# Two graph layers on one core: the second adjacency's exchange moved into the last slots of h1's tile, and the start-up order around it

## The chip, the cores and the metric

The kernel runs on one core of one Trainium2 chip. The metric is device time in microseconds for one execution over the whole batch of 32 graphs; lower is better. The core's engines appear as PE (matrix multiply), PEld (its weight load), DVE (vector), ACT (scalar, activation), POOL (GpSimd) and SP (which here only issues DMAs). Each engine works through its own list of instructions in the order in which the program wrote them; semaphores hold an instruction back until what it needs is there.

## What is computed

For each of 32 graphs with 512 nodes and 512 features, in float32:

```python
h = max(layernorm(x), 0)
agg = (adj @ h) / max(adj.sum(-1), 1e-6)
x = x + relu(concat([h, agg]) @ W.T)            # layer 0
h1 = max(layernorm(x), 0)
q, k = split(h1 @ Wqk); v = h1 @ Wv
w = rowsum(q * (adj @ (k * mask))) * mask / sqrt(512)
x = x + softmax(w over the nodes) * v            # layer 1
```

## The kernel before

Every 512 x 512 product is made with seven products of 256 x 256 quarters instead of eight (Strassen's scheme in Winograd's form). A function `product` emits them in the order M1, M2, M6, M5, M7, M3, M4. One such M with one pair of operands is a **block** of eight matmuls on PE. Each operand is a tile of seven slots: four quarters, and three sums which DVE makes in place with four additions (`left_sums`, `right_sums`; sum 0 fills slot 4, sum 1 slot 6, sum 2 slot 5, sum 3 rewrites a quarter). M1 and M2 need quarters alone; M6 is the first that needs a sum (slot 5).

The stages of a graph b are:

- **y_b** (`layer0_y`): h times the second half of W; seven blocks, result Y.
- **o_b** (`layer0_out`): h times the first half of W, plus adj times Y; each M has two blocks (first h with a streamed weight tile `w1`, then aT with Y), 14 blocks in all.
- **u_b** (`layer1_u`): adj times the masked h1; seven blocks, result U.
- **tv** (`layer1_tv`): h1 times the joined weights of layer 1.

An operand that has to be turned is normalized or scaled on ACT, written to DRAM by row chunks (four DMAs), read back by an **exchange** (four DMAs for each half: `sh..`, `sa..` tiles from the `s` buffers, of which there are two) and then turned on DVE (`turn`). For adj the turned tile is `aT`, for h `hT`, for h1 `h1T`. The tile `aT` is one buffer, shared by all graphs: the first half of its turn (quarters 0 and 1) can be written once M1 and M2 of the stage before have read them, the second half after M4.

The order is written out by hand. `run(phase, n, plan)` emits one block, then the functions that the plan holds under this step's number, then goes on with the product's own code. So a copy or an addition that belongs to an M is emitted after the plan of the step in which its block was emitted. For example, in u the copy of M5's bank (`m5`) is emitted after the plan of step 3 and before M7; in o, with two blocks an M, the copy of M7's bank comes after the plan of step 9. PE accumulates M7 and M4 into the bank `pp`, and M5 and M3 into `pq`: M4 waits for the copy of M7's bank, and M3 for that of M5's.

Four short buffers (`block`, tag `tmp`) hold `m5` and other scratch. In y_1 they also hold the four normalized chunks of graph 0's h1 (`write` in `start`), in the order chunk 0, chunk 1, m5, chunk 2, chunk 3.

The diff touches the start-up: graph 0's stages, written out in `start`, and the first turn of the loop that follows (i = 1: the stage o_1). The pieces to know are:

- `late`, the start's scratch in the buffer of h1T (7 x 7 x 128 per partition): early operands of the weight product, the mask, an identity.
- `fb`, graph 1's adjacency (`FrontA(1)`): loaded and scaled in o_0, chunks written at steps 9 to 12, exchange and first turn in u_0, second turn at step 0 of o_1.
- `f`, graph 0's h1 (`FrontH1(0)`): exchange in y_1, turned and summed in u_0.
- `fd`, graph 2's x (`FrontH(2)`): loaded at step 13 of o_0 into the two `n` half tiles that `fb` leaves, statistics at step 0 of u_0, then `shift` (DVE, makes the bias of the normalization) and `write` (ACT normalizes, SP issues the DMA).
- `fa` in the loop, graph 2's adjacency (`FrontA(2)`): `load`, `sum` (ACT, row sums), `degrees` (DVE), `write`.
- `weights`: additions of 128 x 1792 on the joined weights of layer 1, needed by the stage tv.
- SP issues nearly all DMAs, in the order of emission.

Of the kernel before, what the change touches and what calls it, by code (L numbers as in the profile page):

```python
# [11 lines left out]
F32 = mybir.dt.float32  # L12
# [4 lines left out]
P = 128  # L17
# [5 lines left out]
def kernel(  # L23
# [13 lines left out]
    C = N // P  # L37
# [7 lines left out]
    big = ctx.enter_context(tc.tile_pool(name="big", bufs=1))  # L45
# [43 lines left out]
    def right_sums(s, on=None):  # L89
        return [  # L90
            lambda: sub(s(4), s(1), s(0), on), lambda: sub(s(6), s(3), s(1), on),
            lambda: sub(s(5), s(3), s(4), on), lambda: sub(s(1), s(2), s(5), on),
        ]

    def of(t):
        return lambda i: t[:, i]
# [68 lines left out]
    def run(phase, n, plan):  # L165

        for i in range(n):
            if phase is not None:
                next(phase)
            for f in plan.get(i, []):  # L170
                f()
        if phase is not None:
            assert next(phase, "end") == "end"
# [32 lines left out]
    def exchange(src, name, t=None, queues=one_queue):  # L206


        if t is None:
            t = big.tile([P, 8, P], F32, tag="s", bufs=2, name=name)  # L210
        for q in range(Q):
            queues[q % 2].dma_start(
                out=t[q * R:(q + 1) * R, :, :], in_=src[:, :, ts(q, P)].rearrange("k r j -> r k j")
            )
        return t
# [5 lines left out]
    X, AT_, DEG, W, Y, H1M, H1T, U, TV, HT = ({} for _ in range(10))  # L221
# [44 lines left out]
    def halves(d):  # L266

        return d.rearrange("(h c) (q r) j -> h (c q) r j", h=2, q=Q)

    class Turned:  # L270
# [10 lines left out]
        def turn(self, h, dst):  # L281
            o = dst[:, 2 * h:2 * h + 2, :, :].rearrange("p a b (k r) -> p k (a b) r", r=R)
            nc.vector.transpose(o, self.s.pop(h).rearrange("p k (c r) -> p k c r", r=R))
# [73 lines left out]
    class FrontH1:  # L357
# [30 lines left out]
            right_sums(of(H1M[self.b]))[i]()  # L388

        def turn(self, h):  # L390
            if h == 0:
                H1T[self.b] = big.tile([P, 7, 7, P], F32, tag="h1T", bufs=1, name=f"h1T_{self.b}")
            for a in range(2):
                self.to.turn_slot(h, a, H1T[self.b][:, 2 * h + a, 0:4, :].rearrange("p i f -> p (i f)"))
# [58 lines left out]
    def layer1_u(b):  # L453
        return product(f"u_{b}", [(AT_[b], right(H1M[b]))], *into(U[b]), seed=b + 1 == B)
# [316 lines left out]
    FH, FA, F1 = {}, {}, {}  # L771
# [5 lines left out]

    def start():

        late = big.tile([P, 7, 7, P], F32, tag="h1T", bufs=1, name="late").rearrange("p s i f -> p (s i f)")  # L780
        identity = held["identity"] = late[:, 5120:5248]
        make_identity(nc, identity)
        still = late[:, 5248:5248 + 512]
# [23 lines left out]
        fa = FA[0] = FrontA(0)  # L807
# [92 lines left out]
        p = Plan()  # L900
# [39 lines left out]
        weights = [right_sums(outer)[k] for k in range(4)] + [right_sums(inner)[k] for k in range(4)]  # L940
# [12 lines left out]
        fb = FA[1] = FrontA(1)  # L953
        p = Plan()
# [41 lines left out]
        p.at(11, fh.turn, 1)  # L996
        p.at(11, fh.sums, 0)
        p.at(11, fh.sums, 2)
        fd = FH[2] = FrontH(2)
        for h in range(2):  # L1000
            p.at(13, fd.load, h)
        f = F1[0] = FrontH1(0)
# [9 lines left out]
        p = Plan()  # L1012
# [23 lines left out]
        p = Plan()  # L1036
        for c in range(C):
            p.at(0, fd.stats, c)
        p.at(0, variance, fd.t)
        p.at(1, f.turn, 0)  # L1040
        p.at(1, fb.to.read, 0)
        p.at(1, f.turn, 1)
        p.at(1, fb.to.read, 1)
        p.at(1, load_x, 1)
        p.at(1, FA[0].factor)
        p.at(2, weights[6])
        r1 = right_sums(of(Y[1]))
        p.at(4, fb.turn, 0)
        p.at(4, r1[0])
        p.at(4, shift, fd.t)  # L1050
        p.at(4, r1[2])
        for c in range(C):
            p.at(5, fd.write, c)
        for k in range(4):
            p.at(5 + k // 2, f.sums, k)
        run(layer1_u(0), 7, p)
        return weights[7:], mv

# [4 lines left out]
    }  # L1063
    with tc.manual_schedule(engines=engines):
        weights, mvR = start()
        post = None
        for i in range(1, B):
            more, last = i + 1 < B, i + 1 == B
            f = F1[i] = FrontH1(i)
            p = Plan()  # L1070
# [12 lines left out]
                p.at(2 + 2 * (k // 2), right_y[k])  # L1083
            if i == 1:
                fa = FA[2] = FrontA(2)
                p.at(2, FH[2].to.read, 0)
                p.at(5, fa.load, 0)
                p.at(5, fa.load, 1)
                for h in range(2):
                    for c in range(2):  # L1090
                        p.at([9, 9, 10, 11][2 * h + c], fa.sum, 2 * h + c)
                        p.at(12 + h, fa.write, 2 * h + c)
                    p.at([10, 11][h], fa.degrees, h)
                for k, g in enumerate(weights):
                    p.at(6 + k, g)
                FH[3] = FrontH(3)
                p.at(13, FH[3].load, 0)
                p.at(13, FH[3].load, 1)
            f1 = F1[i - 1]
            if i > 1:  # L1100
                for k in range(4):
                    p.at(k // 2, f1.sums, k)
            if post is not None:
                for c in range(C):
                    p.at(2 + c, post.apply, c)
# [6 lines left out]
            if 1 < i and i + 2 < B:  # L1112
                fh = FH[i + 2]
                late = i == 2
# [12 lines left out]
            if 1 < i and i + 2 < B:  # L1127
                fa = FA[i + 2] = FrontA(i + 2)
# [8 lines left out]
            p = Plan()  # L1137
# [19 lines left out]
            if i == 1:  # L1157
                fa = FA[3] = FrontA(3)
# [32 lines left out]
            p = Plan()  # L1191
# [40 lines left out]
            if more:  # L1232
                p = Plan()
                fb = FA[i + 1]
# [24 lines left out]
        p = Plan()  # L1259
# [11 lines left out]
        p = Plan()  # L1271
# [39 lines left out]
```

## Time and profile before

| | |
|---|---|
| time, median of 3 runs | 2265.5 us (2265.22 to 2266.66) |
| time of the profiled execution | 2267.41 us |
| its span, first to last instruction | 2265.6 us |
| DVE busy | 1913.5 us (84%) |
| ACT busy | 1025.6 us (45%) |
| bytes moved by DMA | 463.69 MB, mean 205 GB/s |
| granted clock of PE | 1.000 over the span |

The span is that of the same execution as the 2267.41 us; 1.8 us lie around it. In a line of the timeline the columns are the start in us from the span's start, the duration in us, the engine (SPq is SP's queue of DMA issues), the source line, the operation, the output and the inputs by tile name, the number of merged instructions, and in brackets how long the engine had been idle just before and what ended it. In the view of waits the columns after the colon are total us, times, and longest us.

### The profile page before, as it was taken

What the parts mean: (1) busy time and instruction counts of PE and PEld (TensorE: products, weight loads), DVE (VectorE), ACT (ScalarE), POOL (GpSimd) and SP (SyncE); (2) the same over time, 40 slices, a digit from 0 to 9 for tenths busy, and PEclk for the clock granted to TensorE, in tenths of its full rate; (3) what the DMA queues carried; (4) which work ended last, traced back from release to release, by engine and by line L of the source; (5) the groups of instructions that cost most, each with busy time, mean ns of one, the idle gap of its engine ahead of it and who ended that gap; (6) DMA issues with size and microseconds to landing.
All of it is one profiled execution on the core that took longest, in us unless ns stands there. A gap on an engine that the chain in (4) does not pass through costs nothing.

```text
span 2265.6 us, 32862 instructions
## 1 busy us (share of the span) xinstructions
PE 2254.2 (99%) x10526; PEld 1981.4 (87%) x10526; DVE 1913.5 (84%) x3778; ACT 1025.6 (45%) x1895; POOL 176.7 (8%) x261
## 2 busy tenths in 40 slices
PE   9999999999999999999999999999999999999999
PEld 7888888888888888888888888888888888888888
DVE  7888888888888888888888888888888888888776
ACT  4364443445434554444454344543454443445323
POOL 0000000000010000000000000001000010000000
PEclk9999999999999999999999999999999999999999
DMA  9978777887878787778878788787778787787644
GB/s 205 252 220 240 210 210 194 204 233 205 210 199 200 214 224 204 203 196 208 229 205 210 193 203 223 218 210 198 193 213 228 203 210 193 206 231 207 155 122 107
DMA packets 409997, 463.69 MB, mean 205 GB/s; under 512 B 38208, under 2 KB 271680, under 8 KB 405600
## 3 DMA queue, kind: packets, MB, share of 16 engines
q1 hardware_dynamic: 396608, 426.46, 69.1%
q0 software_dynamic: 8928, 32.51, 8.6%
q10 hardware_dynamic: 4288, 2.62, 0.6%
q8 instruction: 83, 1.36, 0.3%
q14 instruction: 90, 0.74, 0.1%
HBM read 293.93 MB, written 167.51 MB: 204 GB/s over the span
## 4 chain that ended last, share of the span: by engine, by line
PE 95%; DMA 3%; DVE 1%; SPq 0%; ACT 0%; issue 0%; POOL 0%; DVEq 0%; ACTq 0%
PE ptv L470 28%; PE pp_o L103 19%; PE pp_u L103 9%; PE pq_o L103 9%; PE pp_y L103 9%; PE pq_u L103 5%; PE pr_o L103 5%; PE pq_y L103 5%; PE pr_u L103 2%; PE pr_y L103 2%; PE pw L521 1%; DMA w<-dw 0%; DMA mv<-in_L_gnn_Wqk_dram 0%; DMA mv<-in_L_gnn_W_dram 0%; DMA a<-in_adj_dram 0%; PE pp_v L103 0%
## 5 line engine op out<-in xcount | busy, mean ns | idle before, releaser
L470 PE MATMUL ptv<-mv,h1T 128*128 128x256 f32 x2940 | 639.4, 379 | 0.0
L470 PEld LDWEIGHTS ptv<-mv,h1T 128*128 128x128 f32 x2940 | 558.6, 190 | 75.9
L74 DVE TENSOR_TENSOR tv<-tv 128x256 f32<-128x256 f32 (+1 forms) x645 | 321.8, 511 | 13.2 <-ACT tv L80 1.5
L80 ACT ACTIVATE tv<-ptv 128x512 f32<-128x512 f32 (+1 forms) x360 | 185.0, 542 | 262.8 <-PE ptv L470 261.6
L103 PE MATMUL pp_u<-h1m,aT 128*128 128x256 f32 x1024 | 241.9, 379 | 0.0
L103 PE MATMUL pp_y<-wide 128*128 128x256 f32 x992 | 234.4, 379 | 0.7 <-ACT y L80 0.7
L103 PE MATMUL pp_o<-y,aT 128*128 128x256 f32 x992 | 234.3, 379 | 0.0
L103 PE MATMUL pp_o<-w,wide 128*128 128x256 f32 x960 | 226.8, 379 | 0.0
L103 PEld LDWEIGHTS pp_u<-h1m,aT 128*128 128x128 f32 x1024 | 194.5, 190 | 26.4
L103 PEld LDWEIGHTS pp_y<-wide 128*128 128x128 f32 x992 | 188.3, 190 | 26.6 <-ACT y L80 1.1
L103 PEld LDWEIGHTS pp_o<-y,aT 128*128 128x128 f32 x992 | 188.4, 190 | 25.6
L103 PEld LDWEIGHTS pp_o<-w,wide 128*128 128x128 f32 x960 | 182.4, 190 | 24.8
L80 ACT ACTIVATE o<-pp_o 128x512 f32<-128x512 f32 x96 | 57.2, 596 | 292.9 <-PE pp_o L103 287.7
L80 ACT ACTIVATE y<-pp_y 128x512 f32<-128x512 f32 x124 | 74.0, 597 | 234.0 <-PE pp_y L103 234.0
L74 DVE TENSOR_TENSOR tv<-ptv,tv 128x512 f32<-128x512 f32 x240 | 139.8, 614 | 43.1 <-PE ptv L470 39.4
L77 DVE TENSOR_TENSOR h1T<-h1T 128x512 f32<-128x512 f32 (+1 forms) x189 | 163.5, 878 | 1.3
L80 ACT ACTIVATE xu<-pp_u 128x512 f32<-128x512 f32 x127 | 75.8, 597 | 193.6 <-PE pp_u L103 193.6
L251 POOL TENSOR_TENSOR rstd<-rstd,mhalf 128x2 f32<-128x2 f32 (+1 forms) x97 | 80.0, 825 | 646.0 <-DVE rstd L250 635.6
L103 PE MATMUL pq_u<-h1m,aT 128*128 128x256 f32 x512 | 120.9, 379 | 0.0
L74 DVE TENSOR_TENSOR tv<-ptv,m_tv 128x512 f32<-128x512 f32 (+1 forms) x120 | 72.0, 622 | 57.0 <-PE ptv L470 56.6
L103 PE MATMUL pq_y<-wide 128*128 128x256 f32 x496 | 117.3, 379 | 0.0
L103 PE MATMUL pq_o<-y,aT 128*128 128x256 f32 x496 | 117.2, 379 | 0.0
(167 smaller groups left out, 3310.2 us busy)
## 6 DMA issues: line engine op xcount, KB each, us to landing
w<-dw SPq DMA_DIRECT2D x217, 256.0 KB, 4.3
a<-in_adj_dram SPq DMA_DIRECT2D x256, 128.0 KB, 3.0
dx<-xu SPq DMA_DIRECT2D x32, 1024.0 KB, 5.0
sh1T<-dh1T SPq DMA_DIRECT2D x256, 128.0 KB, 3.4
shT<-dhT SPq DMA_DIRECT2D x248, 128.0 KB, 5.8
daT<-a SPq DMA_DIRECT2D x124, 256.0 KB, 3.0
saT<-daT SPq DMA_DIRECT2D x248, 128.0 KB, 3.4
xu<-in_x_dram SPq DMA_DIRECT2D x124, 256.0 KB, 5.4
```

The costliest lines, as they stand in the source:

```text
L74: (on or nc.vector).tensor_tensor(o, a, b, op=ALU.add)
L77: (on or nc.vector).tensor_tensor(o, a, b, op=ALU.subtract)
L80: nc.scalar.activation(o, i, AF.Copy)
L103: nc.tensor.matmul(p[:, rc, :], lt[:, LEFT[k], dk, ts(rc, P)], right[:, dk, :], start=first and rc == 0 and dk == 0, stop=True, skip_group ...
L251: nc.gpsimd.tensor_tensor(rstd[:, a:b], rstd[:, a:b], mhalf[:, a:b], op=ALU.pow)
L470: nc.tensor.matmul(banks[n][:, :, ts(i, P)], left[:, LEFT[k], LEFT_IN[j], :], mvR[:, RIGHT[k], RIGHT[j], :, :], start=first and i == 0, st ...
L521: nc.tensor.matmul(banks[n][:, ts(i, P)], left[:, LEFT[k], LEFT_IN[j], :], mvR[:, RIGHT[k], RIGHT[j], which, :], start=first and i == 0, s ...
```

## The change

1. `late` becomes graph 0's h1T tile itself: it is made once, and h1's turn writes into it, without a new allocation.
2. The exchange of the second adj (`read_a`, 8 DMAs) moves from step 1 of u_0 to step 13 of o_0, ahead of `fd.load`, and lands in the last slots of that tile (its elements 3584 to 5631) instead of the `s` buffers.
3. h1's four sums, whose results go into these slots, move from u_0 (steps 5 and 6) to o_1 (steps 0 and 1), after the second turn of adj, which reads them free.
4. In u_0 the first turn of adj and `shift` go to step 2, ahead of the two turns of h1 (which go from step 1 to step 2); the four `fd.write` go from step 5 to step 3; `weights[6]` from step 2 to step 5.
5. In o_1 the read of graph 2's h goes from step 2 to 1, the first load of the third adj from step 5 to 3, its row sums from steps 9, 9, 10, 11 to 10, 10, 11, 11, and `degrees` from 10, 11 to 11, 12.

```diff
         def turn(self, h):
-            if h == 0:
+            if h == 0 and self.b > 0:
                 H1T[self.b] = big.tile([P, 7, 7, P], F32, tag="h1T", bufs=1, name=f"h1T_{self.b}")
...
-        late = big.tile([P, 7, 7, P], F32, tag="h1T", bufs=1, name="late").rearrange("p s i f -> p (s i f)")
+        H1T[0] = big.tile([P, 7, 7, P], F32, tag="h1T", bufs=1, name="late")
+        late = H1T[0].rearrange("p s i f -> p (s i f)")
...
+        def read_a(h):
+            room_a = late[:, 3584 + 1024 * h:3584 + 1024 * (h + 1)].rearrange("p (k f) -> p k f", f=P)
+            fb.to.s[h] = exchange(halves(fb.to.d)[h], f"saT_1_{h}", room_a)
+
+        for h in range(2):
+            p.at(13, read_a, h)
         fd = FH[2] = FrontH(2)
...
-        p.at(1, f.turn, 0)
-        p.at(1, fb.to.read, 0)
-        p.at(1, f.turn, 1)
-        p.at(1, fb.to.read, 1)
         p.at(1, load_x, 1)
         p.at(1, FA[0].factor)
-        p.at(2, weights[6])
         r1 = right_sums(of(Y[1]))
-        p.at(4, fb.turn, 0)
+        p.at(2, fb.turn, 0)
+        p.at(2, shift, fd.t)
+        for c in range(C):
+            p.at(3, fd.write, c)
+        p.at(2, f.turn, 0)
+        p.at(2, f.turn, 1)
         p.at(4, r1[0])
-        p.at(4, shift, fd.t)
         p.at(4, r1[2])
-        for c in range(C):
-            p.at(5, fd.write, c)
-        for k in range(4):
-            p.at(5 + k // 2, f.sums, k)
+        p.at(5, weights[6])
         run(layer1_u(0), 7, p)
...
-                p.at(2, FH[2].to.read, 0)
-                p.at(5, fa.load, 0)
+                p.at(1, FH[2].to.read, 0)
+                p.at(3, fa.load, 0)
                 p.at(5, fa.load, 1)
                 for h in range(2):
                     for c in range(2):
-                        p.at([9, 9, 10, 11][2 * h + c], fa.sum, 2 * h + c)
+                        p.at(10 + h, fa.sum, 2 * h + c)
                         p.at(12 + h, fa.write, 2 * h + c)
-                    p.at([10, 11][h], fa.degrees, h)
+                    p.at(11 + h, fa.degrees, h)
...
-            if i > 1:
-                for k in range(4):
-                    p.at(k // 2, f1.sums, k)
+            for k in range(4):
+                p.at(k // 2, f1.sums, k)
```

## The prediction, made before the changed kernel ran

> **What bounds the kernel now.** The page's engine shares come first, then the view of PE's waits.
>
> ```profile
> PE 2254.2 (99%) x10526; PEld 1981.4 (87%) x10526; DVE 1913.5 (84%) x3778; ACT 1025.6 (45%) x1895; POOL 176.7 (8%) x261
> ...
> PE pp_o L103 <- ACT o L80: 2.1, 1, 2.1
> ...
> PE pp_o L103 <- DVE aT L283: 1.1, 1, 1.1
> ...
> PE pp_o L103 <- DVE aT L77: 0.5, 1, 0.5
> ```
>
> PE sets the time, and only 11.4 us of its span are idle. The change can win only idle time of PE, and it touches three waits, all in o_1. The timeline shows them with their causes:
>
> ```profile
> 88.90 1.89 PE L103 MATMUL pp_o<-w,tv 128*128 128x256 f32 x8
> 90.58 1.25 DVE L283 STREAM_TRANSPOSE aT<-saT 128x1024 f32<-128x1024 f32 x1 [2.51 <-DMA saT<-daT]
> ...
> 91.88 1.99 PE L103 MATMUL pp_o<-tv,aT 128*128 128x256 f32 x8 [1.09 <-DVE aT L283]
> ...
> 99.52 1.99 PE L103 MATMUL pp_o<-tv,aT 128*128 128x256 f32 x8 [0.47 <-DVE aT L77]
> ...
> 112.09 0.63 ACT L333 ACTIVATE a<-a 128x512 f32<-128x512 f32 x1 [6.45 <-DMA a<-in_adj_dram]
> ...
> 113.33 0.57 ACT L80 ACTIVATE o<-pp_o 128x512 f32<-128x512 f32 x1
> ...
> 113.96 1.99 PE L103 MATMUL pp_o<-w,tv 128*128 128x256 f32 x8 [2.09 <-ACT o L80]
> ```
>
> First wait: M1's second block needs the first turn of adj, and the exchange had not landed. Second: M6's second block needs slot 5, summed after the second turn. Third: M4 needs M7's bank copied, and on ACT that copy stood behind row sums of a load that had not landed.
>
> **What these waits cost in all.** Unhindered blocks start every 1.727 us (eight starts from 76.81 to 88.90, over 7). From the block at 88.90 to tv's first matmul at 117.52 are 14 blocks, 24.18 us; they took 28.62. The waits and the restarts after them cost **4.44 us**, 0.196%: the most that the change can bring.
>
> **The change, part by part.** *Early exchange, first turn at step 2:* saT lands around 72 us and the turn runs in u_0, long before 90: the first wait goes. *Second turn:* it needs u_0's M4 done, then 1.17 us for it and 0.6 for each of two sums; in the new order DVE has only r1's two sums, one addition, `weights[6]` (1.9) and another addition between h1's turns and it. I walk DVE's list with the trace's starts: the sums end about 2.6 us before M6 wants them without any delay, and with the delays below (which hold PE too) some 6 us before. The second wait goes. h1's sums (2.6 us) come into o_1 behind these; inner sums and `weights[7]`, needed by tv, end about 110 where tv starts at 119: no cost. *Row sums at steps 10 and 11:* the copy after step 9 now stands ahead of them; the third wait goes. The tv copies behind the row sums (four of 0.6) and four scalings (2.6) come some 4 us after these would end. Sum so far: -4.44.
>
> **Price one, in y_1: SP's queue.** `read_a` adds eight issues ahead of `fd.load` and of everything SP issues in y_1.
>
> ```profile
> 65.95 3.63 SPq L204 DMA_DIRECT2D n<-in_x_dram  x8
> ...
> 69.86 1.05 SPq L382 DMA_DIRECT2D dh1T<-h  x2
> ...
> 72.78 1.52 ACT L261 ACTIVATE h<-xu,nmr,rstd 128x512 f32<-128x512 f32 x2
> ...
> 74.21 0.57 ACT L80 ACTIVATE tv<-pp_y 128x512 f32<-128x512 f32 x1
> ...
> 75.09 1.89 PE L103 MATMUL pp_y<-wide,tv 128*128 128x256 f32 x8
> 75.12 4.37 SPq L212 DMA_DIRECT2D sh1T<-dh1T  x8
> ...
> dh1T<-h SPq DMA_DIRECT2D x4, 256.0 KB, 3.1
> ```
>
> The last line (DMA view: size, median us to landing) belongs to the write of h1's chunks. Eight exchange issues take 4.37 (sh1T here). `read_a` waits for the same landing of daT as the load at 65.95 did, so the loads run 70.3 to 73.9 and the first write of h1 goes out at 73.9 instead of 69.86. Who waits: the short buffers. Chunk 3 is the fifth tile taken from four buffers, so it gets chunk 0's, and ACT's fourth normalization must wait until chunk 0 has landed in DRAM: before 69.86 + 3.1 = 73.0, just ahead of its start at 73.5; now 73.9 + 3.1 = 77.0. Behind it on ACT stands the copy of M7's bank (0.72 later), and M4 waits for that. Before, the copy ended at 74.78, with 0.25 to spare (0.06 for the semaphore). So M4 starts at 77.05 + 0.72 + 0.57 + 0.06 = 78.4 instead of 75.09: 3.3, and 0.1 for the restart. Issues after a queue's pause ran longer (the first three of sh1T took about 0.6), so I take **3.6**. Lower end: eight issues at their shortest (0.30 each) move the write by 2.4 only, cost 1.7. Upper end: each read lands after 5.7 (slowest saT) and the loads wait for them, the write itself takes 5.3 (the next graph's): 8.1. The rest of SP's order has cover: h1's exchange, then the weight stream at about 83 instead of 79.5, landing 5.1 later, before o_1 asks for it.
>
> **Price two, in u_0: the normalization of the third x.**
>
> ```profile
> 82.19 0.60 ACT L80 ACTIVATE xu<-pp_u 128x512 f32<-128x512 f32 x1 [2.86 <-PE pp_u L103]
> ...
> 83.92 0.60 ACT L80 ACTIVATE m_u<-pq_u 128x512 f32<-128x512 f32 x1 [1.13 <-PE pq_u L103]
> ...
> 85.45 1.89 PE L103 MATMUL pq_u<-h1m,aT 128*128 128x256 f32 x8
> ...
> 92.51 2.93 ACT L261 ACTIVATE n<-n,nmr,rstd 128x512 f32<-128x512 f32 x4 [6.26 <-DVE nmr L255]
> ```
>
> The last line shows ACT standing 6.26 us for `shift`; there it did so behind M7's copy. At step 3 the four normalizations stand ahead of the copy of M5's bank, for which M3 waits. On DVE `shift` now follows the statistics (end 82.74), one addition (0.60) and the turn (1.17): done at 84.66. ACT: start 84.7, four in 2.83 (92.51 to the next copy's 95.34), copy 0.57, semaphore 0.06: M3 at 88.16 instead of 85.45, 2.7. Price one moves this DVE chain too (the masks stand behind the same copy), by about 0.2 less than PE: 2.5 with a 0.1 restart, **2.6**. Bounds: 2.4 if PE was held longer, 3 if the turn waits on a read. The third x itself lands by 78.5 (73.9 plus 4.6, the slowest), before its statistics.
>
> **Sum:** -4.44 + 3.6 + 2.6 = +1.8 us. The span is 2265.6 in an execution of 2267.41, above the median of 2265.5; I set the difference on the median: **2267.3 us**, 0.08% longer. By its bounds this case reaches from 2265.4 (1.7 and 2.6) to 2272 (8.1 and 3).
>
> A rule of the Trainium skill speaks against it as well. The longest wait quoted above, 2.09 us, left the granted clock at 1.00. "TensorE: Matmul & The Clock Gate", Part 1, says that about 3.4 us without work can halve the clock until it has been busy as long again. A wait of 3.5 us is at that edge; by that page's figures a drop would add an estimated 1.7 to 3.4 us, and the sum would be 2269 to 2270.7; no row of this trace shows such a drop, so I do not add it.
>
> **Rivals.**
> 1. *No new wait:* ACT and SP have enough room, and the three waits are simply gone: 2265.5 - 4.4 = 2261.1. For it: ACT is busy 45%. Against: its order is fixed, and both copies have under 1.3 us of slack.
> 2. *The exchange costs nothing in y_1*, because the write of h1's chunk 0 lands in time; only price two stays, 2.8 alone: 2263.9. For it: SP stands 2.2 us before the second pair of writes. Against: that gap lies behind the first write, which is what counts.
> 3. *Slower: the queue's depth.* In the view of SP's waits a load into a free tile waited for unrelated reads:
>
> ```profile
> SPq L195 <- DMA saT<-daT: 0.9, 3, 0.4
> ```
>
>  SP seems to hold an issue until the eighth before it has landed. Then x's eight loads wait one by one for the eight reads, and the first write slips further. It decides from price one = 4.53 + 4.44 - 2.6 = 6.4 us on, that is a landing of chunk 0 at about 80. With reads of 5.1 (saT's median), issued by 70.3 at the latest, the last load goes at about 75, the write at 75.5, landing 3.1 to 5.3 later: price 5.2 to 7.4. With 6.9: 2270.4. Against: the reads start on queues just drained, where sh1T landed in 3.2 to 3.9.
> 4. *It doesn't do what it says:* the third adj still lands after its new place, M4 waits as before: 2.3 us come back, 2269.6. Against: the load's issue rises from step 5 to 3 and the normalizations ahead of it end earlier.
>
> **How the numbers follow.** A measurement of this kernel can tell about 0.2% (4.5 us) from no change. Chances: both prices near my sizes 0.70; rival 1 0.06; rival 2 0.07; rival 3 0.13; rival 4 0.04. Same gets the forecast (all but 0.03 of it, its upper tail), rivals 2 and 4 and a third of rival 1, together 0.80; slower 0.16; faster 0.04, since even the full gain stands at the limit. The range 2263.0 to 2271.0 leaves out rival 1 and about half of rival 3 and the upper tail.
>
> **What will show it.** The view of PE's waits should have lost the three waits of o_1 and gained two: pp_y on ACT's copy tv (about 3.4 us, at 75 to 78.5) and pq_u on ACT's copy m_u (about 2.5 us). SP should show eight saT reads at about 66, the n loads at 70, the first dh1T at 74. ACT should stand before the fourth normalization of h1 until dh1T lands, and before the four of n until nmr. I am wrong if chunk 3 does not wait for chunk 0's landing, if m_u is copied at once after M5, or if any of the old three waits is there.

## The result, and the profile after

The changed kernel takes 2269.66 us (median of 22 runs, 2268.49 to 2271.03); the kernel before takes 2265.69 beside it (22 runs, 2264.22 to 2266.86). The ratio is 1.0017, interval 1.0011 to 1.0024. It got about 4 us slower; 1.8 were forecast, and 2269.66 lies inside the range of 2263.0 to 2271.0. The profiled execution of the changed kernel has a span of 2267.4 us.

PE's waits in the changed kernel, largest first (total us, times, longest us):

```profile
PE pp_y L103 <- ACT tv L80: 3.2, 1, 3.2
PE pq_u L103 <- ACT m_u L80: 2.2, 1, 2.2
```

All three waits of o_1 are gone from the list; two others stand at its head. The timeline of the changed kernel shows the first of the two being made (start, duration, engine, line, operation):

```profile
65.19 3.77 SPq L212 DMA_DIRECT2D late<-daT  x8
...
69.00 3.74 SPq L204 DMA_DIRECT2D n<-in_x_dram  x8
...
72.90 0.97 SPq L382 DMA_DIRECT2D dh1T<-h  x2
...
77.35 0.81 ACT L261 ACTIVATE h<-xu,nmr,rstd 128x512 f32<-128x512 f32 x1 [3.97 <-DMA dh1T<-h]
78.07 0.57 ACT L80 ACTIVATE tv<-pp_y 128x512 f32<-128x512 f32 x1
...
78.70 1.99 PE L103 MATMUL pp_y<-wide,tv 128*128 128x256 f32 x8 [3.20 <-ACT tv L80]
```

Read it downwards: the eight exchange issues push the third x's eight loads from 66 to 69, these push h1's first write from 69.9 to 72.9; ACT stands for that write's landing, then copies M7's bank, and only then can M4 start. The second wait, a little later in the same timeline:

```profile
87.92 0.12 DVE L255 SCALAR_TENSOR_TENSOR nmr<-mv,rstd 128x4 f32<-128x4 f32 x1
...
88.07 2.93 ACT L261 ACTIVATE n<-n,nmr,rstd 128x512 f32<-128x512 f32 x4 [1.57 <-DVE nmr L255]
...
90.91 0.57 ACT L80 ACTIVATE m_u<-pq_u 128x512 f32<-128x512 f32 x1
...
91.53 1.99 PE L103 MATMUL pq_u<-h1m,aT 128*128 128x256 f32 x8 [2.21 <-ACT m_u L80]
```

The bank of M5 had been complete since about 87.6, but its copy stood behind four normalizations, and these behind `nmr`.

A sum can be made from the starts of PE's blocks alone. From y_1's first block to tv's first matmul there are 28 blocks, 48.36 us at 1.727 each. What a kernel takes beyond that is lost between those points:

| profiled execution | y_1 starts | tv starts | lost, us |
|---|---|---|---|
| before (the one shown first) | 64.73 | 117.52 | 4.43 |
| changed | 64.97 | 119.27 | 5.94 |

The difference is 1.5 us, and the start-up before y_1 was 0.24 us longer: that is the 1.8 us between the two spans. It is not the 4.0 us between the medians. So two questions were left: whether the two waits come from where the prediction put them, and where the other 2 us are.

### The profile page after: what moved, and what is told of

Same layout as the page of the kernel before. It is cut to its first block, busy times and chain, and to the rows that moved or that the text cites. A ratio compares the mean times of both kernels' runs of the same rounds, so it can differ in the third digit from the quotient of the medians.

```text
span 2267.4 us, 32863 instructions
## 1 busy us (share of the span) xinstructions
PE 2254.1 (99%) x10526; PEld 1981.2 (87%) x10526; DVE 1913.0 (84%) x3778; ACT 1025.4 (45%) x1895; POOL 175.2 (8%) x261
## 4 chain that ended last, share of the span: by engine, by line
PE 96%; DMA 2%; DVE 1%; SPq 1%; ACT 0%; issue 0%; ACTq 0%; POOL 0%; DVEq 0%
PE ptv L470 28%; PE pp_o L103 19%; PE pp_u L103 10%; PE pq_o L103 9%; PE pp_y L103 9%; PE pq_u L103 5%; PE pr_o L103 5%; PE pq_y L103 5%; PE pr_u L103 2%; PE pr_y L103 2%; PE pw L521 1%; DMA mv<-in_L_gnn_Wqk_dram 1%; DMA mv<-in_L_gnn_W_dram 0%; SPq L212 0%; DMA dh1T<-h 0%; PE pp_v L103 0%
## 5 line engine op out<-in xcount | busy, mean ns | idle before, releaser
L470 PE MATMUL ptv<-mv,h1T 128*128 128x256 f32 x2842 | 618.2, 379 | 0.0
L470 PEld LDWEIGHTS ptv<-mv,h1T 128*128 128x128 f32 x2842 | 539.9, 190 | 73.5 <-DVE xu L449 0.2
L77 DVE TENSOR_TENSOR h1T<-h1T 128x512 f32<-128x512 f32 (+1 forms) x183 | 158.1, 877 | 1.2
```

Of the source, the lines that this page charges most:

```text
L77: (on or nc.vector).tensor_tensor(o, a, b, op=ALU.subtract)
L470: nc.tensor.matmul(banks[n][:, :, ts(i, P)], left[:, LEFT[k], LEFT_IN[j], :], mvR[:, RIGHT[k], RIGHT[j], :, :], start=first and i == 0, st ...
```

## The experiments

The kernels 1 to 4, 5 to 8 and 9 to 12 were timed side by side, each group with its own runs of the kernel before, whose medians were 2266.51, 2266.51 and 2266.90 us; so ratios are compared, not times.

**1. The kernel before once more** (no edit).

> The kernel before, unchanged, profiled once more. The medians of before and changed kernel differ by 4.0 us, the two profiled executions by only 1.8, and the profiled execution of before took 2267.4 where its runs lie at 2265.7. Theory: that execution had unusually long waits in o_1 (4.44 us lost there); a usual one loses about 2.0 to 2.7 us there, so this profile shows a span of about 2264 and tv starting about 115.1 to 115.8 instead of 117.5. Rival: the waits of o_1 are always 4.4 us and the 2 us lie elsewhere in the span or around it; then tv starts again at 117.2 to 117.8. Both expect a ratio of 1.000 against itself, within 0.0007.

Ratio to itself 0.9994 (0.9985 to 1.0003), span of the profiled execution 2264.1. Its waits:

```profile
PE pp_o L103 <- ACT o L80: 1.7, 1, 1.7
...
PE pp_o L103 <- DVE aT L77: 0.5, 1, 0.5
```

y_1 at 64.75, tv at 115.94: 2.83 lost, not 4.43. The first wait is absent. This chain of the same profile's timeline shows why:

```profile
88.92 1.89 PE L103 MATMUL pp_o<-w,tv 128*128 128x256 f32 x8
89.36 1.25 DVE L283 STREAM_TRANSPOSE aT<-saT 128x1024 f32<-128x1024 f32 x1 [1.92 <-DMA saT<-daT]
90.66 1.99 PE L103 MATMUL pp_o<-tv,aT 128*128 128x256 f32 x8
```

The exchange landed 1.2 us earlier than in the first profile (turn at 89.36 instead of 90.58), and the turn just fits before M1's second block. The theory held in the main, with 2.83 slightly above its 2.0 to 2.7: the first profile of before was slower than the usual execution. At 2267.41 us it lies above all 22 runs of the result. It is not rare, though: of the 87 runs of before beside the experiments, 30 took 2267.4 us or more. Which waits those had was not profiled.

**2. Exchange behind h1's first writes.**

```diff
-        for h in range(2):
-            p.at(13, read_a, h)
...
         p.at(1, f.keep)
+        for h in range(2):
+            p.at(1, read_a, h)
         p.at(4, write, 2)
```

> The changed kernel with the exchange of the second adj issued in y_1, behind the first two writes of h1 and x1's, instead of ahead of the third x's load. Theory: chunk 0 of h1 lands about 73 as before, PE's wait for the copy tv in y_1 (3.2 us) is gone and the one for m_u (2.2 to 2.6 us) stays; the saT reads land by about 80, before the turn at 83. Time 2269.7 - 3.4 = 2266.3, ratio to before 1.0003. Rival: it is not the place in the queue but the added megabyte beside the write that delays it; then at least 1 us of the wait for tv stays, and the time is 2267.3 or more.

2266.36 us, ratio 1.0000 (0.9991 to 1.0009). The waits of y_1 and u_0 that are left:

```profile
PE pq_u L103 <- ACT m_u L80: 1.9, 1, 1.9
```

The same megabyte is now issued from 70.87 on, behind h1's first write. That write goes out at 69.26 again and lands after 3.0 us, and the wait for tv is gone. In the changed kernel it goes out at 72.90 and takes 4.4 us to land. So both parts of the delay, the later issue and the slower landing, come from what stands ahead of it in SP's list; this experiment does not take the two apart. Against the changed kernel's 1.0017 the removal is worth 3.9 us. That is 0.5 more than expected, well inside the interval, which is 2 us to either side.

**3. Normalizations of the third x back at step 5.**

```diff
         for c in range(C):
-            p.at(3, fd.write, c)
+            p.at(5, fd.write, c)
```

> The changed kernel with the four normalizations of the third x back at step 5 of u_0, behind the copies of M5's and M7's banks. Theory: the wait for m_u is gone, the one for tv in y_1 (3.2 us) stays: 2269.7 - 2.5 = 2267.2, ratio 1.0007. Rival: the third x is then written some 3 us later, the third adj's load waits for its half tiles, and M4 of o_1 waits again for M7's copy or tv for ACT: 1 us or more comes back there, 2268.2 or more.

2268.60 us, ratio 1.0009 (1.0000 to 1.0018). The wait for m_u is gone and none of o_1 returns. But the one for tv was 3.9 us in this profile, and a new thing shows behind it; it is taken up under number 8. The time comes near the rival's 2268.2, but not by the rival's cause, since nothing comes back in o_1. The removal is worth 1.8 us, 0.7 less than expected and again inside the interval.

**4. Both edits.**

> Both edits at once: exchange behind the first writes of h1, normalizations at step 5. Theory: neither new wait, and none of the three old ones in o_1: 2269.7 - 3.4 - 2.5 = 2263.8, ratio to before 0.9991, span about 2262. Rival: the 2.2 us by which the medians differ more than the profiles are a cost of the change outside these two waits; then this version stands at or above 2265.7.

2264.28 us, ratio 0.9991 (0.9982 to 1.0000). y_1 at 64.86, tv at 113.21: 48.35 us, nothing lost. The rival falls: there is no further cost in the change outside the two waits.

**5. A buffer of its own for h1's chunk 3**, the exchange left where the change put it.

```diff
         def write(c):
-            f.write(c, block(f"h1_{f.b}_{c}"))
+            own = late[:, 5632:6144].rearrange("p (a f) -> p a f", a=2)
+            f.write(c, own if c == 3 else block(f"h1_{f.b}_{c}"))
```

> The changed kernel, exchange still ahead of the third x's load, but the fourth normalized chunk of h1 goes into free space of the late tile (elements 5632 to 6143) and so needs no short buffer. Theory: PE's wait for the copy tv in y_1 (3.2 us) is gone although the first write of h1 still goes out at about 73 and lands at about 77, because only the shared buffer tied ACT to it; the wait for m_u stays and may grow a little, since h1's turn and the rest of SP's order are still late. Ratio to before 1.0000 to 1.0004. Rival: M4 of y_1 or M1 of u_0 is held by something else behind the late queue (masks, h1's exchange, the weight stream); then 1 us or more of wait stays in y_1, u_0 or the start of o_1, and the ratio is 1.0008 or more.

2265.83 us, ratio 0.9998 (0.9989 to 1.0006): as expected, or a little better. The timeline of its profiled execution (at 2268.94 us the slowest of its 11) shows the fourth normalization free and a different one held:

```profile
74.03 0.80 ACT L261 ACTIVATE late<-xu,nmr,rstd 128x512 f32<-128x512 f32 x1
74.13 0.95 SPq L382 DMA_DIRECT2D dh1T<-h  x2
...
75.32 0.32 SPq L371 DMA_DIRECT2D dx<-xu  x1
...
83.01 0.60 ACT L80 ACTIVATE xu<-pp_u 128x512 f32<-128x512 f32 x1 [4.72 <-DMA dx<-xu]
...
83.66 3.44 PE L103 MATMUL pp_u<-h1m,aT 128*128 128x256 f32 x8 [2.55 <-ACT xu L80]
```

ACT normalizes chunk 3 at 74.03, before the first write is even issued, so it was the shared buffer that tied ACT to SP's queue. But U takes the place of x, and its first copy must wait until x has been stored (`dx`, also issued late): M6 of u_0 waited 2.5 us for it here. Both theories have a part: the wait named is removed, and in this execution the next transfer behind the same queue was late. The wait for m_u did not stay at 2.2 us, as the theory had it; it was 0.5.

**6. The exchange read twice**, the second time into unused space: 16 issues ahead instead of 8.

```diff
         for h in range(2):
             p.at(13, read_a, h)
+        for h in range(2):
+            p.at(13, lambda h=h: exchange(
+                halves(fb.to.d)[h], f"again_{h}",
+                late[:, 1024 * h:1024 * (h + 1)].rearrange("p (k f) -> p k f", f=P)))
```

> The changed kernel with the exchange of the second adj read a second time, into unused space of the late tile: 16 issues ahead of the third x's load instead of 8. Theory: the price follows the issues ahead of the first write, 3.8 us for eight; the wait for tv grows from 3.2 to about 7 us, and so long a gap also lowers the granted clock in every execution (half of it for 6.8 us after a wait of 3.9 us in the kernel with the normalizations at step 5): 2269.7 + 3.8 + 2.4 = 2275.9, ratio 1.004 to 1.005. Rival: the wait is set by the landing of the data and not by the issues, so reads of data already on their way add little: 2271 or less, ratio under 1.0025.

2275.64 us (5 runs), ratio 1.0039 (1.0027 to 1.0052). The time is as expected, but two misses cancel in it: the wait for tv was 9.1 us, not 7, and the wait for m_u shrank to 0.5, which the sum had left at 2.2.

```profile
66.09 7.72 SPq L212 DMA_DIRECT2D late<-daT  x16
...
73.85 4.77 SPq L204 DMA_DIRECT2D n<-in_x_dram  x8
...
78.98 0.86 SPq L382 DMA_DIRECT2D dh1T<-h  x2
```

The view of SP's waits in this profile has a line for the loads, and that of the first profile of the changed kernel one for h1's writes (total us, times, longest us):

```profile
SPq L204 <- DMA late<-daT: 1.9, 6, 0.4
...
SPq L382 <- DMA n<-in_x_dram: 0.6, 3, 0.2
```

The first write of h1 went out 6.1 us later than in the changed kernel (78.98 instead of 72.90). Sixteen issues took 7.72, twice the 3.77 of eight: 3.95 of the 6.1 follows the number of issues. The queue also started 0.9 later in this execution (66.09 instead of 65.19), and the loads took 4.77 instead of 3.74. This last part is a matter of landing, as the rival had it. Each of the eight loads, and the write behind them, went out within 0.1 us after the eighth issue before it had landed. For example, the ninth read was issued at 69.90 and landed after 3.9, and the first load was issued at 73.85; that load landed after 5.1, and the write was issued at 78.98. No issue in this stretch came before that landing. The changed kernel, with eight issues, only touches this limit: x's first load was issued at 69.00 and landed after 3.8, and the write, held by it for at most 0.2 us, was issued at 72.90. In the kernel before the write was issued 1.4 us after that landing.

**7. The later row sums alone**, in the kernel before.

```diff
-                        p.at([9, 9, 10, 11][2 * h + c], fa.sum, 2 * h + c)
+                        p.at(10 + h, fa.sum, 2 * h + c)
...
-                    p.at([10, 11][h], fa.degrees, h)
+                    p.at(11 + h, fa.degrees, h)
```

> The kernel before with one part of the change alone: in o_1 the third adj's row sums at steps 10, 10, 11, 11 and degrees at 11, 12. Theory: the third wait (1.7 to 2.1 us, 2 to 2.3 with the restart) is gone, the second (0.5) and sometimes the first stay: 2265.7 - 2.0 = 2263.7, ratio 0.9991. Rival: with the load still at step 5 the data lands at about 112, ACT stands there for the row sums while tv's first copies queue behind them, and PE waits in tv for a bank: 1 us or more comes back, ratio 0.9996 or more.

2263.87 us, ratio 0.9990 (0.9981 to 0.9999). The timeline of its ACT in o_1:

```profile
106.88 0.60 ACT L80 ACTIVATE o<-pp_o 128x512 f32<-128x512 f32 x1 [2.81 <-PE pp_o L103]
110.68 0.63 ACT L333 ACTIVATE a<-a 128x512 f32<-128x512 f32 x1 [3.20 <-DMA a<-in_adj_dram]
```

M7's bank is copied as soon as it is complete; ACT then stands for the third adj, and nobody on PE waits for that. y_1 at 65.24, tv at 113.59: nothing lost, the first two waits were not there in this execution.

**8. The changed kernel once more**, for the clock.

> The changed kernel once more, unchanged, on the same chip as its variants. Theory: ratio 1.0017 again (1.0012 to 1.0022); the profile shows a wait of 3 to 4 us for tv in y_1 and of 2 to 2.6 for m_u; where the first is over about 3.5 us the granted clock stands at half for 6.8 us behind it and some 2.4 us more are lost, which a fifth of the first 22 runs show by a mean clock of 0.998. Rival: the clock has nothing to do with the wait; then it stays at 1.00 behind a wait of any length.

2269.80 us, ratio 1.0014 (1.0005 to 1.0023). The wait for tv was 4.1 us, the one for m_u only 0.5. The view of four stretches of 3.4 us of this profile (columns: stretch, length, busy us of PE, PEld, DVE, ACT, POOL, then PE's granted clock, DMA share, GB/s):

```profile
72.75:76.16 3.41, 2.50 (x12) 1.87 (x10) 2.25 (x2) 0.56 (x1) 0.00 (x0) 1.00 1.08 230
76.17:79.57 3.40, 0.17 (x1) 0.18 (x2) 0.20 (x1) 1.52 (x3) 0.00 (x0) 1.00 1.05 397
79.59:82.99 3.40, 3.40 (x9) 2.65 (x9) 3.26 (x6) 0.98 (x2) 0.00 (x0) 0.50 1.07 342
83.00:86.41 3.41, 3.41 (x18) 3.00 (x17) 3.31 (x8) 1.19 (x2) 0.00 (x0) 1.00 1.13 194
```

After a stretch in which PE was busy for 0.17 us the clock stood at 0.50 for one stretch: PE was busy all the time but did 9 matmuls instead of 18. In the first profile of the changed kernel the clock stayed at 1.00 behind a wait of 3.2 us. The rival falls. Two details of the theory were wrong here: the drop lasted 3.4 us and not 6.8, and the wait for m_u was not 2 to 2.6.

**9 to 12. What the parts bring.** The version of experiment 4 without the edits in o_1 (early exchange only), then experiments 7 and 4 again, and a third profile of the kernel before.

```diff
-                p.at(1, FH[2].to.read, 0)
-                p.at(3, fa.load, 0)
+                p.at(2, FH[2].to.read, 0)
+                p.at(5, fa.load, 0)
...
-                        p.at(10 + h, fa.sum, 2 * h + c)
+                        p.at([9, 9, 10, 11][2 * h + c], fa.sum, 2 * h + c)
...
-                    p.at(11 + h, fa.degrees, h)
+                    p.at([10, 11][h], fa.degrees, h)
```

> The kernel with both new waits taken out (exchange behind h1's first writes, normalizations at step 5), and with the edits of o_1 undone too: load at 3 back to 5, read of graph 2's h back to 2, row sums back to 9, 9, 10, 11. What is left is the early exchange with the turns and sums that go with it. Theory: the first and second wait are gone for good, the third (1.7 to 2.1 us) is back; as the first two cost only 0.6 us in the second profile of before and nothing in that of the kernel with later sums, the ratio is 0.9996 to 1.0000. Rival: the exchange is the main gain (1.36 + 0.74 us in the first profile of before); then the ratio is 0.9990 or less.

> The kernel before with the later row sums alone, once more. Theory: ratio 0.9990 again (0.9986 to 0.9994), since its profile has no loss left between y_1 and tv. Rival: its profile was a lucky one, and the first or second wait is usually there; then it is 0.4 us or more above the kernel with all edits and neither new wait.

> The changed kernel without its two new waits, once more, beside the one-part version. Theory: 0.9990 (0.9986 to 0.9994), within 0.3 us of the version with the later sums alone. Rival: what the exchange saves shows as 0.5 us or more between the two.

> The kernel before, a third look at its waits in o_1. Theory: the third wait is there again (1.5 to 2.2 us), the first comes and goes with the landing of the exchange (0 to 1.1 us): 2.2 to 4.5 us lost in all. Rival: the first profile of before shows the usual case; then 4.2 to 4.7 us.

| kernel | ratio to before | interval | y_1 starts | tv starts | lost, us |
|---|---|---|---|---|---|
| early exchange only | 1.0000 | 0.9991 to 1.0009 | 64.46 | 115.01 | 2.19 |
| later row sums only | 0.9989 | 0.9980 to 0.9997 | 64.86 | 113.65 | 0.43 |
| all, without the two new waits | 0.9990 | 0.9981 to 0.9999 | 65.32 | 113.67 | 0 |
| before, third profile (one time, 2265.58 us) | | | 64.68 | 115.46 | 2.42 |

The early exchange, the part that needed most of the diff, brings nothing that can be measured; the row sums bring it all (about 2.4 us). The rival of 9 falls. Those of 10 and 11, 0.4 to 0.5 us between the two better versions, are not supported, since these lie at 2264.23 and 2264.41 us, 0.2 apart; but the intervals are too wide to exclude them, or any gain of the exchange under about 2 us. In the third profile of before the third wait is 1.9 us, the first is absent. Both versions are faster than the kernel before and than the changed one; their intervals end just below 1, in one of four measurements at 1.0000.

## Why the prediction was right, and where its size was off

*The three old waits go*: right, each of them, with tv's operands ready as walked through.

*Price one, the queue*: right in place and kind, 3.6 forecast, about 3.5 found in the first profile (M4 at 78.70 instead of 75.09 + 0.24, and 0.1 for the restart: a block behind a wait takes 1.99 us instead of 1.89). That the size came out so well is luck, since two errors in it cancelled: the exchange took 3.77 us of SP and not 4.37, and started earlier, so the write went out at 72.90 and not at 73.9; but it took 4.4 us to land (72.90 to 77.3), not the 3.1 of the kernel before. Experiments 2, 5 and 6 test the place, the shared buffer and the number of issues.

*Price two, ACT's order*: right, 2.6 forecast, 2.36 between the start of M3 at 91.53 and its due time (85.45, 0.24 and 3.48 later), with a restart 2.5. Experiment 3 removes it alone.

*Saving of 4.44 us*: this is the mis-sized term. It was read off one execution, and then its difference was set on the median of the runs. That execution took 2267.41 us where the runs lay at 2265.5; the prediction saw the gap and did not ask whether the extra time stood in the very waits it was about to subtract. It did: three profiles of before lost 4.43, 2.83 and 2.42 us between y_1 and tv, and only the first has the wait for the exchange. With the two shorter ones the sum is 3.6 + 2.6 - 2.6 = +3.6, and 4.0 was measured. Experiments 4 and 11 measure the term itself: with both prices taken out, the changed kernel is 2.0 to 2.5 us faster than the kernel before (ratios 0.9991 and 0.9990, each to about 2 us), not 4.44.

*The clock*: the page "TensorE: Matmul & The Clock Gate", Part 1, was weighed and left out of the sum. It should have been a part of it with a chance: the drop to half the clock appeared in one of two profiles of the changed kernel and in those of experiments 3, 5 and 6. Among the first 22 runs the four slowest (2270.40 to 2271.03 us) are those with a mean clock of 0.998. How many more had a drop, the means don't tell: the execution of experiment 8, with a drop of one stretch, shows 0.999, and so does a profile of before that had none between y_1 and tv. A drop adds to price one and takes from price two. In experiment 8 the block before M3 of u_0 starts 2.4 us later than in the first profile (89.82 instead of 87.44), but M3 itself only 0.7 (92.24 instead of 91.53): what M3 waits for was hardly later, so the wait was 0.5 instead of 2.2. Over the runs, however, the two prices add up as forecast, as far as can be measured: taking out the first was worth 3.9 us, the second 1.8, both 5.9 (each to about 2 us), and 6.2 was forecast.

*Rivals*: rival 1 and 2 fell with the first profile; rival 4 as well. Rival 3, the queue's depth, is real: with eight added issues it held h1's first write by 0.2 us at most, with sixteen it set the time of every load and of the write (experiment 6).

Left open: why the exchange lands 1 to 2 us later in some executions of the kernel before than in others. Most of the difference is the time from issue to landing: its median was 5.1 us in the first profile of before, 4.4 and 3.6 in the other two, while the first read was issued at 84.07, 83.59 and 83.61. What made the landing slower is not shown.

## What to carry to other kernels

Moving a transfer earlier on a shared queue moves everything behind it later: list what it overtakes, and for each of these who waits for its landing, buffers that come free only then included. The same holds for an engine's own list: an operation that waits must not stand ahead of a copy that PE needs within a microsecond. And before a wait is subtracted from the median, look whether the profiled execution is itself as long as the median; if it is not, the wait may be where it differs.

## What the hardware showed that was not expected

"TensorE: Matmul & The Clock Gate", Part 1, speaks of an idle window of about 3.4 us before the clock falls. Here it fell behind a shorter wait. This is the view of stretches of experiment 5, where PE's wait was 2.5 us:

```profile
79.80:83.20 3.40, 1.31 (x7) 0.80 (x5) 3.23 (x9) 0.19 (x1) 0.00 (x0) 1.00 1.01 369
83.22:86.62 3.40, 2.96 (x7) 2.43 (x8) 2.31 (x5) 0.38 (x1) 1.18 (x2) 0.50 0.75 165
```

And this one is of the first profile of the changed kernel, with a wait of 3.2 us:

```profile
73.90:77.30 3.40, 1.59 (x8) 1.06 (x6) 0.68 (x1) 0.00 (x0) 0.00 (x0) 1.00 1.06 291
77.30:80.70 3.40, 2.00 (x9) 1.80 (x10) 1.92 (x4) 2.52 (x4) 0.00 (x0) 1.00 1.01 416
80.70:84.10 3.40, 3.40 (x17) 2.99 (x17) 3.32 (x6) 1.19 (x2) 0.00 (x0) 1.00 1.20 249
```

And these are of experiment 3, with a wait of 3.9 us:

```profile
73.90:77.31 3.41, 1.35 (x7) 0.84 (x5) 1.17 (x1) 0.00 (x0) 0.00 (x0) 1.00 1.06 273
77.33:80.73 3.40, 1.55 (x4) 1.28 (x5) 1.57 (x3) 2.52 (x4) 0.00 (x0) 0.50 1.02 420
```

The stretches are laid where the trace's own record of the clock changes, in steps of 3.413 us. Where PE was busy 1.31 us of 3.40 in one of them, the clock fell in the next; where a longer wait lay across two of them, with 1.59 and 2.00 busy in each, it did not. Over all such stretches of the 14 profiles, from about 5 us after the start to the end, the longest busy time with a drop behind it is the 1.35 us of experiment 3; the shortest without one is 1.44 us (experiment 6, at the end of its span, 2268.2 to 2271.6). So in these runs it was the busy share of a fixed stretch that decided, somewhere between 40% and 42%, and not the length of the wait. For the way back the same share was not enough: at half clock, stretches with 1.55 us busy (the last line above) and 2.47 us (experiment 6, 83.65 to 87.06) were followed by another at half clock, and those with 2.96 us and more by one at full clock. One stretch at half clock costs, by estimate, 1.7 us (9 matmuls of 18 in 3.4 us, experiment 8); whether a wait of 3 us costs that much more is a matter of where it falls.
